# Self attention in a three-part Perceiver layer: the values' share token-major inside the logits' loop, and Ev turned by VectorE

## The chip, the cores and the metric

The kernel runs on one core of a Trainium2 chip. The metric is the device time of one execution in microseconds (us). Engines are written as in the profile: PE is TensorE (its weight loads are PEld), DVE is VectorE, ACT is ScalarE, POOL is GpSimd, SP is SyncE. L727 is line 727 of the kernel before.

## The reference

Three residual sub-layers on `x` (4 batches, 128 tokens, 512 channels, 16 heads of 32 channels), all in f32: a cross attention over 2048 context tokens whose softmax runs over the heads, a self attention with relative positions, and a cosine-like self attention with routed gates. Only the second is touched by the change:

```python
def _L0_attn_ref(x, Wq, Wk, Wv, Eq, Ek, Ev):     # x is layer-normalised
    r = jnp.arange(S)
    rel = jnp.clip(r[:, None] - r[None, :], -MAX_DIST, MAX_DIST) + MAX_DIST
    q, k, v = (proj(Wq), proj(Wk), proj(Wv))
    a_q, a_k, a_v = Eq[rel], Ek[rel], Ev[rel]
    content = jnp.einsum('bhld,bhmd->bhlm', q, k)
    rel_k = jnp.einsum('bhld,lmd->bhlm', q, a_k)
    rel_q = jnp.einsum('bhmd,lmd->bhlm', k, a_q)
    pos_pos = jnp.einsum('lmd,lmd->lm', a_q, a_k)
    logits = (content + rel_k + rel_q + pos_pos) * scale
    attn = jax.nn.softmax(logits, axis=-1)
    out = jnp.einsum('bhlm,bhmd->bhld', attn, v) + jnp.einsum('bhlm,lmd->bhld', attn, a_v)
    return out.transpose(0, 2, 1, 3).reshape(B, S, D)
...
x = x + _L0_attn_ref(_layernorm(x), ...)
x = x + _L0_ffn_ref(_layernorm(x), ...)
```

The second term of `out` is called Ev below: for every token position p, the attention weights of all heads and batches times a window of the table Ev.

## The kernel before

The kernel has three stages, one for each sub-layer. Within a stage the order of instructions is written out by hand (`manual_schedule`): every engine executes its own queue in the order of the program text, and semaphores between the engines are put in automatically. There is no planner, so what an engine does next is what the text says next, and an instruction that waits holds up everything behind it on its engine. Stage 1 (cross attention) lasts to about 650 us and isn't touched.

Stage 2 is the self attention. The 16 heads are handled in four chunks `c` of `NH` = 4 heads (128 channels), and every chunk head has its 4 batches side by side, so that one PSUM bank holds 4 x 128 = 512 columns. First q, k, v and the two relative terms are computed; `rk` and `lg` hold them. Then a loop over `c` does this for each chunk:

- `logits(c)` (L683): PE turns 16 blocks of `rk` into PSUM (L687) and adds the q k products (L700). It takes four banks, the only four of its pool, so logits of the next chunk wait until the joins have read them.
- `join(c)` (L713): four DVE additions of a PSUM bank to `lg` (L716).
- `largest(c, i)` (L720): the negated row maximum, one DVE instruction for each head.
- `exponentials_of(c, i)` (L724): four ACT exponentials for each head with their row sums (L727).
- `softmax(c, i)` (L731): a DVE reciprocal (L733) and a POOL multiplication by it (L734).
- `transposed(c, i)` (L738): PE turns the four 128x128 blocks of a head into a PSUM bank (L742), and DVE (heads 0 and 1) or ACT (heads 2 and 3) copies it to `eT` (L743).

In the loop before, `logits(c + 1)` stands first in pass c, and the turns of chunk c - 1 are spread behind the joins of chunk c + 1. After the loop, `attend(c)` (L750) makes the values' share of each chunk channel-major: it first turns four blocks of the residual `x1` into the bank (L753) and then adds 16 products with 32 columns of `v` as weights and 128 columns of `eT` moving (L765), four column groups of PE beside each other. DVE copies the bank to `oT` (L773). Then Ev: 128 positions, each one product with a 32-column window of the table as weights and the 64 columns of `eT` at that position moving (L818), in four groups of 32 positions. Its result has channels of one head on 32 partitions and positions, heads and batches along the free side, so it is brought into `oT` in strips of 32 partitions: half by ACT copies to `oev` (L835) with a POOL addition (L839), half by DVE additions (L833). Finally 16 PE turns bring `oT` back to tokens (L843), and `layernorm_T` (L145) takes the statistics (L157, L158), normalises (L161, L169, L165), turns the result into `xT` (L214, L215) and copies the new residual to `x1` (L207).

Stage 3 begins with `queries(b)` (L888) for each batch b: four 512-column products (L227), a DVE addition of the bias row (L891) and an ACT square (L893); `lengths(b)` (L896) and `normalised(b)` (L900) follow. Its bias rows are loaded by POOL's queue (L52) once stage 2's memory is free. After the queries come `keys` (L220) and the rest of the gated attention.

PSUM has eight banks. In stage 2, four belong to the logits (freed after the loop), three to `bank`, one to `bank_z`; stage 3 splits them into four for `bank_l` and four for `bank`.

Of the kernel before, what the change touches and what calls it, by code (L numbers as in the profile page):

```python
# [9 lines left out]
F32 = mybir.dt.float32  # L10
AF = mybir.ActivationFunctionType
# [5 lines left out]
def perceiver_layer(ctx: ExitStack, tc: tile.TileContext, a: dict, out: bass.AP):  # L17
# [7 lines left out]
    nc = tc.nc  # L25
# [210 lines left out]
    with s1:  # L236
# [11 lines left out]
        def bank(n):  # L248
            return ps_g.tile([P, 512], F32, tag="ps", name=f"ps_{n}")
# [318 lines left out]
    with ExitStack() as s2:  # L568
# [11 lines left out]
        def bank_z(n):  # L580
            return psz.tile([P, 512], F32, tag="psz", name=f"s2_{n}")
# [101 lines left out]
        def logits(c):  # L683
            ps, _ = banks(f"l{c}")
            for i in range(NH):
                for b in range(B):
                    nc.tensor.matmul(  # L687
                        ps[i][:, b * T : (b + 1) * T],
                        lhsT=rk[:, (c * NH + i) * B + b, :],
                        rhs=ident,  # L690
                        is_transpose=True,
                        start=(b == 0),
                        stop=False,
                        skip_group_check=True,
                    )
            for b in range(B):
                cols = slice(b * T, (b + 1) * T)
                for i in range(NH):
                    rows = slice(i * HD, (i + 1) * HD)
                    nc.tensor.matmul(  # L700
                        ps[i][:, cols],
                        lhsT=qT[rows, c, cols],
                        rhs=kT[rows, c, cols],
                        start=False,
                        stop=True,
                        skip_group_check=True,
                    )
            return ps
# [1 line left out]
        def of_head(c, i):  # L710
            return slice((c * NH + i) * B, (c * NH + i + 1) * B)

        def join(c, ps):  # L713
            for i in range(NH):
                fs = of_head(c, i)
                nc.vector.tensor_tensor(  # L716
                    lg[:, fs, :], ps[i].rearrange("p (b m) -> p b m", b=B), lg[:, fs, :], ALU.add
                )
# [9 lines left out]
                    lg[:, f, :], lg[:, f, :], AF.Exp, bias=nm[:, f : f + 1], accum_out=rs[:, f : f + 1]  # L728
                )

        def softmax(c, i):  # L731
            fs = of_head(c, i)
            nc.vector.reciprocal(rs[:, fs], rs[:, fs])  # L733
            nc.gpsimd.tensor_tensor(  # L734
                lg[:, fs, :], lg[:, fs, :], rs[:, fs].unsqueeze(2).to_broadcast([P, B, T]), ALU.mult
            )

        def transposed(c, i):  # L738
            ps = bank(f"t{c}_{i}")
            fs = of_head(c, i)  # L740
            for b in range(B):
                nc.tensor.transpose(ps[:, b * T : (b + 1) * T], lg[:, fs.start + b, :], ident)  # L742
            (nc.scalar.copy if i >= 2 else nc.vector.tensor_copy)(  # L743
                eT[:, fs, :], ps.rearrange("p (b l) -> p b l", b=B)
            )


        oT = one.tile([P, C, B, T], F32, tag="qT", name="oT2")

        def attend(c, eng):  # L750
            ps = bank_z(f"o{c}") if c % 2 else bank(f"o{c}")
            for b in range(B):
                nc.tensor.matmul(  # L753
                    ps[:, b * T : (b + 1) * T],
                    lhsT=x1[:, b, c * P : (c + 1) * P],
                    rhs=ident,
                    is_transpose=True,
                    start=(b == 0),
                    stop=False,
                    skip_group_check=True,  # L760
                )
            for b in range(B):
                for i in range(NH):
                    h = c * NH + i
                    nc.tensor.matmul(  # L765
                        ps[i * HD : (i + 1) * HD, b * T : (b + 1) * T],
                        lhsT=v[:, b, h * HD : (h + 1) * HD],
                        rhs=eT[:, h * B + b, :],
                        start=False,
                        stop=True,  # L770
                        skip_group_check=True,
                    )
            eng(oT[:, c].rearrange("p b l -> p (b l)"), ps)  # L773

        ps = logits(0)
        join(0, ps)
        for i in range(NH):
            largest(0, i)
        for c in range(C):
            if c + 1 < C:  # L780
                ps = logits(c + 1)
            for i in range(NH):
                exponentials_of(c, i)
            if c + 1 < C:
                join(c + 1, ps)
            for i in range(NH):
                if c + 1 < C:
                    largest(c + 1, i)
                softmax(c, i)
                if c:  # L790
                    transposed(c - 1, i)
        s2_loop.close()
        psq = s2.enter_context(tc.tile_pool(name="s2_psq", bufs=4, space=PSUM))

        def bank_q(n):
            return psq.tile([P, 512], F32, tag="psq", name=f"s2_{n}")


        nc.scalar.activation(small.tile([P, 1], F32, tag="rt", name="rt2"), eps, AF.Sqrt)
        attend(0, nc.vector.tensor_copy)  # L800
        attend(1, nc.vector.tensor_copy)
        for i in range(NH):
            transposed(C - 1, i)
            if i == 1:
                attend(2, nc.vector.tensor_copy)

        oev = one.tile([P, C * B, NG4, J8], F32, tag="kT", name="oev")  # L810
        by_8 = oT.rearrange("p c b (g n j) -> p (c b) g n j", g=NG4, j=J8)
        for n in range(NJ // J8):
            bk8 = bank_q(f"ev{n}")
            ps = bk8.rearrange("p (j f) -> p j f", f=NF)
            for j in range(J8):
                for g in range(NG4):
                    p = NJ * g + n * J8 + j
                    nc.tensor.matmul(  # L818
                        ps[g * HD : (g + 1) * HD, j, :],
                        lhsT=ev_win[:, T - 1 - p, :],  # L820
                        rhs=eT[:, :, p],
                        start=True,
                        stop=True,
                    )
            if n == 0:
                attend(C - 1, nc.vector.tensor_copy)
            for g in range(NG4):
                from_ = ps[g * HD : (g + 1) * HD].rearrange("p j (c i b) -> p i c b j", i=NH, b=B)
                for i in range(NH):
                    rows = slice(i * HD, (i + 1) * HD)  # L830
                    if n % 2:
                        to = oT[rows, :, :, g * NJ + n * J8 : g * NJ + (n + 1) * J8]
                        nc.vector.tensor_tensor(to, from_[:, i], to, ALU.add)  # L833
                    else:
                        nc.scalar.copy(  # L835
                            oev[rows].rearrange("p (c b) g j -> p c b g j", b=B)[:, :, :, g, :], from_[:, i]
                        )
            if n % 2 == 0:
                nc.gpsimd.tensor_tensor(by_8[:, :, :, n, :], by_8[:, :, :, n, :], oev, ALU.add)  # L839
        out_ps = [bank_q(f"out{b}") for b in range(B)]  # L840
        for b in range(B):
            for c in range(C):
                nc.tensor.transpose(out_ps[b][:, c * P : (c + 1) * P], oT[:, c, b, :], ident)  # L843
        xT = layernorm_T(out_ps, ps1, 2)

# [8 lines left out]
    with ExitStack() as s3:  # L854
# [121 lines left out]
        def attend(c, eng):  # L976
# [11 lines left out]
                    )  # L988
            eng(oT[:, c, :], ps)

        sqs = {0: queries(0)}
        for b in range(B):
            lengths(b, sqs[b])
            if b + 1 < B:
                sqs[b + 1] = queries(b + 1)
            normalised(b)
# [178 lines left out]
```

## Time and profile before

| what | value |
|---|---|
| median of 3 runs | 875.72 us (874.93 to 877.7) |
| the profiled execution | 875.97 us |
| its span, first to last instruction | 874.1 us |
| busy: PE, DVE, ACT, POOL | 830.6 (95%), 628.2 (72%), 436.5 (50%), 430.6 (49%) us |
| mean granted TensorE clock | 0.98 of full speed |
| first exponential of stage 2 | 732.25 us |
| Ev's products | 768.08 to 779.23 us |
| stage 3's queries on PE | 793.97 to 807.94 us |

Times inside the span are counted from its first instruction. Lines of the trace give start, duration, engine, source line, operation, output <- inputs, shapes and a count; in square brackets stands how long the engine was idle before it and what ended that. PE executes an f32 product in two records with a weight load each, so 16 products appear as x32; a turn (transpose) is one record. Busy shares are averages over stages that have different limits.

### The profile page before, as it was taken

The page shows a single profiled execution, that of the slowest core. Times are in us where ns is not written, and L with a number is a line of the kernel's source. Part 1 is how long each engine was busy: PE and PEld are TensorE (multiplying, and loading weights), DVE is VectorE, ACT ScalarE, POOL GpSimd, SP SyncE. Part 2 cuts the span into 40 slices and gives each one's busy share as a digit, 9 for nine tenths or more (in the row PEclk, how much of TensorE's full clock was granted, in tenths as well). Part 3 has the DMA queues.
Part 4 walks back from the last instruction along what each step waited for, and adds up shares of the span by engine and source line. Part 5 has one row for each costly group of instructions (what it writes and reads, how often), then busy time and mean ns, then how long its engine had stood idle before and what let it go on. Part 6 is the DMA issues. An engine that isn't in the chain of part 4 may idle for free. (4 is left out here: it accounts for less than half of the span.)

```text
span 874.1 us, 16373 instructions
## 1 busy us (share of the span) xinstructions
PE 830.6 (95%) x7061; PEld 447.9 (51%) x7061; DVE 628.2 (72%) x616; ACT 436.5 (50%) x721; POOL 430.6 (49%) x289
## 2 busy tenths in 40 slices
PE   9999999999999999999999999999898997779998
PEld 5454544554544545445445445544443466664564
DVE  2059788878888888888889888788861637556663
ACT  3357455564464554554554555644411736843671
POOL 1236666566656567575675665667500002512152
PEclk9999999999999999999999999999998998798999
DMA  8130010110101101010010101010100212001101
GB/s 300 50 124 2 1 49 1 49 49 1 50 1 49 49 2 49 1 49 13 37 49 1 49 1 49 1 36 15 49 28 21 96 50 98 1 2 51 49 1 49
DMA packets 10905, 35.53 MB, mean 41 GB/s; under 512 B 977, under 2 KB 1138, under 8 KB 8786
## 3 DMA queue, kind: packets, MB, share of 16 engines
q1 hardware_dynamic: 8402, 29.43, 9.7%
q10 hardware_dynamic: 1632, 3.15, 1.1%
q0 software_dynamic: 800, 1.93, 0.9%
q8 instruction: 55, 0.90, 0.4%
q14 instruction: 16, 0.13, 0.0%
HBM read 33.45 MB, written 1.05 MB: 39 GB/s over the span
## 5 line engine op out<-in xcount | busy, mean ns | idle before, releaser
L328 DVE TENSOR_TENSOR sg<-sg,stat 128x2048 f32<-128x2048 f32 x128 | 288.2, 2282 | 1.2
L337 ACT ACTIVATE sg<-sg 128x2048 f32<-128x2048 f32 x64 | 122.4, 1912 | 246.8 <-DVE sg L328 246.8
L227 PE MATMUL ps_v<-w_xattn_Wv,ct 128*128 128x512 f32 x512 | 231.5, 596 | 3.7 <-ACT v L274 3.7
L220 PE MATMUL ps_k<-ct,w_xattn_Wk 128*128 128x512 f32 x480 | 221.9, 605 | 0.8 <-ACT pos L142 0.8
L343 POOL TENSOR_TENSOR sm<-sm,sg 128x1024 f32<-128x1024 f32 x46 | 108.6, 2360 | 145.5 <-ACT sg L337 143.3
L307 DVE TENSOR_TENSOR mx<-mx,ps_s 128x1024 f32<-128x1024 f32 x96 | 117.2, 1221 | 78.1 <-ACT sg L298 65.9
L227 PEld LDWEIGHTS ps_v<-w_xattn_Wv,ct 128*128 128x128 f32 x512 | 95.8, 190 | 129.9 <-issue 113.5
L220 PEld LDWEIGHTS ps_k<-ct,w_xattn_Wk 128*128 128x128 f32 x480 | 86.2, 189 | 94.1 <-issue 86.1
L298 ACT COPY sg<-ps_s 128x1024 f32<-128x1024 f32 x128 | 124.2, 1020 | 7.2 <-DVE mx L305 3.5
L344 POOL TENSOR_TENSOR sm<-sm,sg 128x1024 f32<-128x1024 f32 x46 | 108.8, 2366 | 3.6
L275 POOL TENSOR_TENSOR v<-v,row_xattn_bv 128x512 f32<-128x512 f32 x64 | 81.6, 1276 | 40.0 <-ACT v L274 40.0
L734 POOL TENSOR_TENSOR lg<-lg,rs 128x512 f32<-128x512 f32 x16 | 16.3, 1041 | 120.9 <-issue 112.3
L285 PE MATMUL ps_s<-qT,kT 32*128 32x128 f32 x2048 | 75.7, 283 | 0.1
L372 PEld LDWEIGHTS pso<-sg,v 128*32 128x32 f32 x1920 | 48.8, 109 | 47.5 <-DVE mx L307 22.0
L285 PEld LDWEIGHTS ps_s<-qT,kT 32*128 32x128 f32 x2048 | 63.3, 186 | 18.0 <-issue 17.0
L372 PE MATMUL pso<-sg,v 128*32 128x128 f32 x1920 | 64.6, 276 | 3.7 <-DVE acc L385 2.1
L341 POOL TENSOR_TENSOR sm<-sg 128x1024 f32<-128x1024 f32 x16 | 37.9, 2366 | 45.3 <-ACT sg L337 45.2
L268 ACT ACTIVATE kT<-ps_k,bk 128x512 f32<-128x512 f32 x64 | 44.2, 694 | 10.4 <-PE ps_k L220 5.9
L274 ACT COPY v<-ps_v 128x512 f32<-128x512 f32 x64 | 36.4, 569 | 8.5 <-PE ps_v L227 8.4
L385 DVE TENSOR_TENSOR acc<-pso,acc 128x512 f32<-128x512 f32 x54 | 37.0, 684 | 3.9 <-PE pso L372 3.9
L305 DVE TENSOR_TENSOR mx<-sg,ps_s 128x1024 f32<-128x1024 f32 x16 | 19.5, 1220 | 27.3 <-ACT sg L298 27.3
L964 POOL TENSOR_TENSOR e<-e,rs 128x512 f32<-128x512 f32 x16 | 16.3, 1041 | 41.8 <-DVE rs L963 41.8
(208 smaller groups left out, 817.0 us busy)
## 6 DMA issues: line engine op xcount, KB each, us to landing
ct<-in_ctxT SPq DMA_DIRECT2D x15, 1024.0 KB, 4.9
ev_win<-in_tabv SPq DMA_DIRECT2D x1, 2048.0 KB, 7.1
w_xattn_Wk<-in_xattn_Wk ACTq DMA_DIRECT2D x4, 256.0 KB, 8.0
ct<-in_ctxT SPq DMA_DIRECT2D x4, 256.0 KB, 6.7
x<-in_x SPq DMA_DIRECT2D x4, 256.0 KB, 8.2
w_xattn_Wv<-in_xattn_Wv ACTq DMA_DIRECT2D x1, 1024.0 KB
w_xattn_Wq<-in_xattn_Wq SPq DMA_DIRECT2D x1, 1024.0 KB, 10.3
w_xattn_Wo<-in_xattn_Wo ACTq DMA_DIRECT2D x1, 1024.0 KB, 5.4
```

Of the source, the lines that this page charges most:

```text
L220: nc.tensor.matmul(ps, lhsT=w[:, k, c * P : (c + 1) * P], rhs=src[:, k, :], start=(k == 0), stop=(k == C - 1))
L227: nc.tensor.matmul(ps, lhsT=src[:, k, b * T : (b + 1) * T], rhs=w[:, k, :], start=(k == 0), stop=(k == C - 1))
L268: nc.scalar.activation(kT[n, c], ps, AF.Identity, bias=bk[:, c : c + 1])
L275: nc.gpsimd.tensor_tensor(v[n, b], v[n, b], bv_row, ALU.add)
L285: nc.tensor.matmul(ps[i][:, cols], lhsT=kT[n, c][rows, cols], rhs=qT[rows, c, cols], start=True, stop=True)
L298: nc.scalar.copy(sg[n, c][:, k * HALF : (k + 1) * HALF], pss[n, c][k])
L307: nc.vector.tensor_tensor(mxs[n], mxs[n], pss[n, c][k], ALU.max)
L328: nc.vector.tensor_tensor(g, g, stat[:, row, :].unsqueeze(1).to_broadcast([P, NH * B, T]), op)
L337: nc.scalar.activation(sg[n, c], sg[n, c], AF.Exp, scale=SCALE)
L343: eng.tensor_tensor(t, t, g[:, 0:HALF], ALU.add)
L344: eng.tensor_tensor(t, t, g[:, HALF:], ALU.add)
L372: nc.tensor.matmul(ps[i * HD : (i + 1) * HD, b * T : (b + 1) * T], lhsT=v[n, b][:, h * HD : (h + 1) * HD], rhs=sg[n, c][:, f * T : (f + 1) ...
```

## The change

- `attend` becomes token-major: for each head and batch one product with the 128 columns of `eT` as weights and 32 columns of `v` moving, into `bank_z`. It can be given some of the heads, and it no longer turns `x1`. `attended(c)` adds the bank to `x1` on DVE.
- In the loop, `logits(c + 2)` is issued near the end of pass c, after the turn of head 1. Of chunk c, heads 0 and 1 are turned in pass c and heads 2 and 3 at the start of pass c + 1; the values' share of chunk c - 1 stands in pass c between the turns of heads 0 and 1. The first joins and row maxima alternate. The last chunk's two late turns are copied by DVE, and its last softmax multiplication is on DVE.
- After the loop Ev's products go to one tile of four banks, the order of positions changed; twelve products with a constant tile follow on PE. DVE turns Ev for each batch in 32x32 blocks to token-major, straight out of PSUM; DVE (batch 0) or POOL (batches 1 to 3) adds it to `x1`. Statistics, root, reciprocal, offset and scaling are done batch by batch, the scaling on ACT.
- Stage 3 turns the normalised batches itself: `x_turned(b + 1)` stands behind `queries(b)`. Strips, `oev`, the 16 turns of `oT` and the copies to `x1` are gone.

```diff
-        def join(c, ps):
-            for i in range(NH):
+        def join(c, ps, heads=range(NH)):
+            for i in heads:
...
-        def softmax(c, i):
+        def softmax(c, i, eng=nc.gpsimd):
...
-        def attend(c, eng):
-            ps = bank_z(f"o{c}") if c % 2 else bank(f"o{c}")
...
+        def attend(c, heads=range(NH), ps=None):
+            if ps is None:
+                ps = bank_z(f"o{c}")
+            for i in heads:
+                for b in range(B):
                     h = c * NH + i
                     nc.tensor.matmul(
-                        ps[i * HD : (i + 1) * HD, b * T : (b + 1) * T],
-                        lhsT=v[:, b, h * HD : (h + 1) * HD],
-                        rhs=eT[:, h * B + b, :],
+                        ps[:, b * T + i * HD : b * T + (i + 1) * HD],
+                        lhsT=eT[:, h * B + b, :],
+                        rhs=v[:, b, h * HD : (h + 1) * HD],
+                        start=True,
+                        stop=True,
+                    )
+            return ps
+        def attended(c, ps):
+            xc = x1[:, :, c * P : (c + 1) * P]
+            nc.vector.tensor_tensor(xc, ps.rearrange("p (b d) -> p b d", b=B), xc, ALU.add)
...
+        act, dve = nc.scalar.copy, nc.vector.tensor_copy
+        ps = logits(0)
+        for i in range(NH):
+            join(0, ps, (i,))
+            largest(0, i)
+        ps = logits(1)
+        for c in range(C):
+            last = c + 1 == C
+            exponentials_of(c, 0)
+            if not last:
+                join(c + 1, ps)
+            softmax(c, 0)
+            if c:
+                transposed(c - 1, 2, dve if last else act)
+                transposed(c - 1, 3, dve if last else act)
+            if not last:
+                largest(c + 1, 0)
+            exponentials_of(c, 1)
+            softmax(c, 1)
+            transposed(c, 0, dve)
+            if not last:
+                largest(c + 1, 1)
+            if c:
+                po = attend(c - 1)
+            exponentials_of(c, 2)
+            softmax(c, 2)
+            if not last:
+                largest(c + 1, 2)
+            transposed(c, 1, dve)
+            exponentials_of(c, 3)
+            if c + 2 < C:
+                ps = logits(c + 2)
+            if c:
+                attended(c - 1, po)
+            if not last:
+                largest(c + 1, 3)
+                softmax(c, 3)
...
+        po = attend(C - 1, (0, 1))
+        transposed(C - 1, 2, dve)
+        softmax(C - 1, 3, nc.vector)
+        transposed(C - 1, 3, dve)
+        attend(C - 1, (2, 3), po)
+        attended(C - 1, po)
+        ev = psq.tile([P, NJ, NF], F32, tag="ev", name="ev")
+        for j in range(NJ):
...
+        for _ in range(12):
+            nc.tensor.matmul(ps, lhsT=warm, rhs=warm, start=True, stop=True)
+        def turn(b):
+            nc.vector.transpose(
+                turned[:, b, :].rearrange("p (h d) -> p h d", d=HD),
+                ev.rearrange("p j (h b) -> p b h j", b=B)[:, b],
+            )
+        def add(b, eng):
+            eng.tensor_tensor(x1[:, b, :], x1[:, b, :], turned[:, b, :], ALU.add)
+        def statistics(b):
+            nc.vector.bn_stats(st[:, b, :], x1[:, b, :])
+            nc.vector.bn_aggr(mv[:, b, :], st[:, b, :])
+            nc.scalar.activation(rstd[:, b : b + 1], mv[:, b, 1:2], AF.Sqrt, bias=eps)
+        def normalised(b):
...
+            nc.scalar.activation(xn[b], x1[:, b, :], AF.Identity, bias=nmr[:, one_], scale=rstd[:, one_])
+        turn(0)
+        add(0, nc.vector)
+        statistics(0)
+        turn(1)
+        add(1, nc.gpsimd)
+        normalised(0)
+        turn(2)
+        add(2, nc.gpsimd)
+        statistics(1)
+        turn(3)
+        add(3, nc.gpsimd)
+        normalised(1)
+        statistics(2)
+        normalised(2)
+        statistics(3)
+        normalised(3)
...
+        def x_turned(b):
+            ps = bank_l(f"xT{b}")
+            for c in range(C):
+                nc.tensor.transpose(ps[:, c * P : (c + 1) * P], xn[b][:, c * P : (c + 1) * P], ident)
+            nc.scalar.copy(xT[:, :, b * T : (b + 1) * T], ps.rearrange("p (c t) -> p c t", c=C))
+        x_turned(0)
         sqs = {0: queries(0)}
         for b in range(B):
+            if b + 1 < B:
+                x_turned(b + 1)
             lengths(b, sqs[b])
```

More of the change, by code (lines that the diff above doesn't have):

```diff
@@ L729, in exponentials_of, with transposed @@
                 )
-        def softmax(c, i):
+        def softmax(c, i, eng=nc.gpsimd):
             fs = of_head(c, i)
             nc.vector.reciprocal(rs[:, fs], rs[:, fs])
-            nc.gpsimd.tensor_tensor(
+            eng.tensor_tensor(
                 lg[:, fs, :], lg[:, fs, :], rs[:, fs].unsqueeze(2).to_broadcast([P, B, T]), ALU.mult
             )
-        def transposed(c, i):
+        def transposed(c, i, eng):
             ps = bank(f"t{c}_{i}")
@@ L742, in transposed @@
                 nc.tensor.transpose(ps[:, b * T : (b + 1) * T], lg[:, fs.start + b, :], ident)
[L743 to L748, printed above, removed]
-        def attend(c, eng):
-            ps = bank_z(f"o{c}") if c % 2 else bank(f"o{c}")
[L752 to L763, printed above, removed]
+            eng(eT[:, fs, :], ps.rearrange("p (b l) -> p b l", b=B))
@@ L764, in attend @@
+        def attend(c, heads=range(NH), ps=None):
[3 more added lines that the diff above has]
+                for b in range(B):
                     h = c * NH + i
                     nc.tensor.matmul(
-                        ps[i * HD : (i + 1) * HD, b * T : (b + 1) * T],
-                        lhsT=v[:, b, h * HD : (h + 1) * HD],
-                        rhs=eT[:, h * B + b, :],
-                        start=False,
-                        stop=True,
@@ L771, in attend @@
[L771 to L805, printed above, removed]
@@ L810, in perceiver_layer @@
[L810 to L821, printed above, removed]
+                        ps[:, b * T + i * HD : b * T + (i + 1) * HD],
@@ L824, in perceiver_layer @@
                     )
-            if n == 0:
-                attend(C - 1, nc.vector.tensor_copy)
-            for g in range(NG4):
[L828 to L844, printed above, removed]
+            return ps
+        def attended(c, ps):
+            xc = x1[:, :, c * P : (c + 1) * P]
+            nc.vector.tensor_tensor(xc, ps.rearrange("p (b d) -> p b d", b=B), xc, ALU.add)
@@ new lines, in perceiver_layer @@
+        s2_loop.close()
+        psq = s2.enter_context(tc.tile_pool(name="s2_psq", bufs=1, space=PSUM))
+        nc.scalar.activation(small.tile([P, 1], F32, tag="rt", name="rt2"), eps, AF.Sqrt)
+        po = attend(C - 1, (0, 1))
[6 more added lines that the diff above has]
+        for j in range(NJ):
+            for g in range(NG4):
+                nc.tensor.matmul(
+                    ev[g * HD : (g + 1) * HD, j, :],
+                    lhsT=ev_win[:, T - 1 - (NJ * g + j), :],
+                    rhs=eT[:, :, NJ * g + j],
+                    start=True,
+                    stop=True,
+                )
@@ new lines, in perceiver_layer @@
+        ps = bank("warm")[:, 0:P]
+        for _ in range(12):
+            nc.tensor.matmul(ps, lhsT=warm, rhs=warm, start=True, stop=True)
+        turned = one.tile([P, B, D], F32, tag="kT", name="evT")
+        def turn(b):
[3 more added lines that the diff above has]
+            )
+        st = small.tile([P, B, 6], F32, tag="st", name="st2")
+        mv = small.tile([P, B, 2], F32, tag="mv", name="mv2")
@@ new lines, in perceiver_layer @@
+        rstd = small.tile([P, B], F32, tag="rstd", name="rstd2")
+        nmr = small.tile([P, B], F32, tag="nmr", name="nmr2")
+        xn = [tmp.tile([P, D], F32, tag="xn", name=f"xn2_{b}") for b in range(B)]
+        def add(b, eng):
[4 more added lines that the diff above has]
+            nc.scalar.activation(rstd[:, b : b + 1], mv[:, b, 1:2], AF.Sqrt, bias=eps)
@@ new lines, in normalised @@
+        def normalised(b):
+            one_ = slice(b, b + 1)
+            nc.vector.reciprocal(rstd[:, one_], rstd[:, one_])
+            nc.vector.scalar_tensor_tensor(
+                nmr[:, one_], in0=mv[:, b, 0:1], scalar=-1.0, in1=rstd[:, one_], op0=ALU.mult, op1=ALU.mult
+            )
+            nc.scalar.activation(xn[b], x1[:, b, :], AF.Identity, bias=nmr[:, one_], scale=rstd[:, one_])
[4 more added lines that the diff above has]
+        add(1, nc.gpsimd)
@@ L989, in attend @@
             eng(oT[:, c, :], ps)
+        xT = tpool.tile([P, C, B * T], F32, tag="xT", name="xT2")
+        def x_turned(b):
[4 more added lines that the diff above has]
+        x_turned(0)
         sqs = {0: queries(0)}
         for b in range(B):
+            if b + 1 < B:
+                x_turned(b + 1)
             lengths(b, sqs[b])
```

## The prediction

> **What bounds the kernel now.** I read the page's slices first, then the chain of waits in order of time, then the timelines of single engines and the windows' granted clock between 715 and 812 us, where all edits lie. Stage 1 ends at 650 us, so its share of the busy time says nothing here.
>
> ```profile
> span 874.1 us, 16373 instructions
> ...
> PE   9999999999999999999999999999898997779998
> ...
> ACT  3357455564464554554554555644411736843671
> ...
> PEclk9999999999999999999999999999998998798999
> ```
>
> Each digit is a fortieth, 21.9 us: slices 33 to 35 (721 to 787 us) are the only ones where PE is not nearly full, and ACT takes over in slice 33. The profiled execution took 875.97 us, 1.87 more than its span and 0.25 more than the median of the three (875.72); the sum below is made against 875.97.
>
> ```profile
> 732.25 12.43 ACT lg L727 x64
> ...
> 768.08 2.52 PE s_ev L818 x60
> ...
> 774.60 0.28 DVE oT L833
> ...
> 784.36 1.10 PE s_out L843 x4
> ...
> 793.97 13.97 PE s_q L227 x32
> ```
>
> That is the chain (start, us, what; 64 counts each exponential and its accumulator read). The loop hangs on ACT's exponentials, the last at 761.1; the position products (Ev) run on PE from 768.08 to 779.23; then come strips on DVE (L833), turns, normalisation, and stage 3's queries from 793.97 to 807.94. From there on nothing is edited. So three marks decide: start of Ev, end of Ev, end of the queries.
>
> **The loop, part by part.** Prices, from the timelines (start, us, engine, line, [idle <-releaser]):
>
> ```profile
> 733.97 2.48 DVE L716 TENSOR_TENSOR lg<-s_l,lg 128x512 f32<-128x512 f32 x4
> 735.41 2.26 PE L687 MATMUL s_l<-ident,rk 128*128 128x128 f32 x16 [1.47 <-DVE lg L716]
> 738.75 0.66 PE L742 MATMUL s_t<-ident,lg 128*128 128x128 f32 x4
> 742.23 1.04 POOL L734 TENSOR_TENSOR lg<-lg,rs 128x512 f32<-128x512 f32 x1 [0.54 <-DVE rs L733]
> 771.12 1.08 PE L765 MATMUL s_o<-eT,v 128*32 128x128 f32 x32
> ```
>
> Four joins 2.4 (start to start); a logits group 3.34 (735.41 to 738.75); a head's turn 0.66; reciprocal (starts 741.98) plus POOL product (ends 743.27) 1.29; a largest or an eT copy on DVE 0.6 to 0.7.
>
> *The values' share.* Before, 16 products with 32 weight columns, four column groups side by side: 32 records, 1.08 us. After, eT is the weight (128 columns) and v moves 32 columns: again 32 records, but no two share the array. No row has this shape. From below it is bounded by the old 1.08; the nearest row with full f32 weights is the warming group of the start, of which a window holds
>
> ```profile
> 4.42:5.49 1.07, 1.07 (x10) 1.07 (x9) 1.00 1.08 374
> ```
>
> ten records in 1.07 us, 0.107 each, with as many weight loads. With 128 columns of weights per record I take 32 x 0.107 = 3.4; from above the same group's mean, 4.62/24 = 0.19, gives 6.2. [...]
>
> *The order.* Engines run their queues in order. In pass c, DVE now has: four joins of c+1, the first reciprocal of c, and only then the largest of c+1 and the eT copies. PE has: turns (c-1,2), (c-1,3), (c,0), the values' share of c-1, turn (c,1), logits c+2. So from the end of one logits group to the end of the next the steps follow each other: joins 2.4, reciprocal and product 1.29, turn 0.66, values' share A, turn 0.55, logits 3.34, some 0.05 of semaphore: 8.3 + A = 11.7 us. Before, logits c+1 stood in front of the turns on PE and the pass took 6.2 to 8.5 (exponentials of passes 0 to 3 begin at 732.25, 738.4, 746.9, 754.9). Nothing covers the difference: ACT's copies of turns (c-1,2), (c-1,3) stand between exponentials (c,0) and (c,1), and those turns wait behind the logits, so ACT stands still too.
>
> Worked through: joins and largest of pass 0 now alternate, a dependent pair costing 1.33, so exponentials start at 730.5 instead of 732.25, but the fourth join ends at 733.8 and logits 1 at 736.1 (before 733.9). Logits 2: joins to 738.5, product (0,0) 739.8, (0,1) 740.8, turn 741.5, logits 744.8. Logits 3: 744.8 + 11.7 = 756.5. Then: product (2,0) 760.3, turn 760.9, values 1 764.3, turn and copy (2,1) 765.6, the add into x1 and largest (3,3) 766.8, products (2,3) 768.1 and (3,0) 769.1, turn 769.8, values 2 773.2, turn and copy (3,1) and add 775.4, half of values 3 777.1, turn and copy (3,2) 778.4, reciprocal and product of (3,3) on DVE 779.3, turn 780.0, copy 780.7, rest of values 3 781.3. Ev starts at 781.3 rather than 768.08. It takes 256 x 0.0377 (7.21 us for 192) = 9.65 as before, without the 1.75 of values 3 in its midst: end 791.0 against 779.23, **+11.8**.
>
> Gone from PE are 16 x1 turns (about 2.6 us) and 16 output turns; they stood after the exponentials, so they are in the sum through the marks.
>
> **After Ev.** Removed: 32 strips on DVE (9.6 us, half beside PE), 32 on ACT, two POOL adds, four copies of x1. Added per batch: a 32x32 turn on DVE, an add, statistics, scaling. The turn is in no row; other 128x512 reads of PSUM on DVE, strided ones too (L634), take 0.69, single-input ones down to 0.66; bounds 0.5 and 1.3 (the POOL add), and I take 0.69. POOL's adds take 1.28 (L458). From Ev's end: turn, add, statistics, root of batch 0 to 2.7; turn 1 ends 3.0; POOL's adds at 4.35, 5.6, 7.3; statistics of batch 1 4.4, of 2 6.1 (behind batch 1's scale on DVE), of 3 7.6; the last root waits for ACT's scaling of batch 2 to 8.55; root, scale, offset 9.2; the last scaling 10.1. Stage 3's first xT copy is behind that on ACT: 10.6. So "each batch by itself" doesn't bring the first query forward by much: PE has batch 0's turn at 4.2 and waits. Then four queries of 3.43, with a new gap between: add 0.69, square 0.63 (ACT), copy of the next xT 0.59, semaphores: 2.0 each, three times. End 30.4 after Ev. The wait also costs clock:
>
> ```profile
> 659.08 5.80 PE L220 MATMUL s_q<-xT,w_attn_Wq 128*128 128x512 f32 x8 [0.83 <-ACT x L207]
> ```
>
> after stage 1's normalisation the first eight records took 5.8, not 3.43: 2.4 more (bounds 0 and 3.4). The twelve warming products end about 2.6 after Ev, 8 us too early. Sum 32.8 against 807.94 - 779.23 = 28.7: **+4.1**. POOL's row loads now queue behind its last add (7.3); bq is landed some 4 us later, before 14.1 where it is used. The exponentials' table in stage 3 and the output weights move along.
>
> **The clock in the loop.**
>
> ```profile
> 741.87:745.28 3.41, 0.00 (x0) 1.00 0.00 0
> 745.28:748.69 3.41, 3.39 (x16) 0.50 0.00 0
> 748.69:752.11 3.41, 3.20 (x50) 1.00 0.00 0
> ```
>
> (window, length, PE busy and records, clock.) An empty window was followed by half clock, a full one by full clock. The same addition made for the old order ends the exponentials at 759.1 where the trace has 761.2, so half-clock stretches and bank waits cost **2.1** there; I carry that over. [...]
>
> Sum: 875.97 + 11.8 + 4.1 + 2.1 = **894.0 us**.
>
> **Rivals.**
> - *Faster.* The pass fits under ACT: 730.5 + 64 x 0.386 + four copies 2.0 = 757.2, tail 3.6 (product, turn, copy, products), Ev 760.8 to 770.5, queries to 803.3: 871.3, with stage 3 ahead of the last scaling on ACT about 866. It decides where the time from logits to logits is under 7.2. For it: ACT starts 1.75 earlier and is what the chain names. Against: 8.3 even with the values' share free. 0.09.
> - *Cheap values' share* (1.1): logits 3 at 754.2, Ev 772.9 to 782.6: 3.4 + 4.1 + 2.1 = 885.6; about 881 if the xT copies pass the scaling. 0.15.
> - *Half clock through the loop*: weights with 32 moving columns keep the array mostly empty. All turns, logits and values at 1.5 times their time end Ev at about 805 instead of 791: 908; at half clock nearly throughout beyond 915. 0.2.
> - *Forecast case*, 888 to 902: 0.56.
>
> **How the numbers follow.** Predicted 894. Range 881 to 912: the lower end is the cheap share, the upper takes in half clock at 1.5; outside are the faster case and the worst clock, about 0.2. What this kernel's measurement tells from no change is about 0.3%. Faster 0.09; of the cheap share's 0.15, where the xT copies also pass the scaling and the clock stays up, 0.03 is put within 0.3%: same 0.03; the rest, slower 0.88.
>
> **What would show it.** Right: values' share groups of 32 records at 3.4 us or more; logits to logits near 12; ACT idle some 4 us before each xT-like copy of turns in passes 1 and 2; Ev starting near 781; first query 10 to 11 us after Ev, at half clock; gaps near 2 between queries. Wrong: values' share near 1.1; exponentials ending by 762; Ev starting before 768; queries starting within 6 us of Ev.

## The result, and the profile after

The changed kernel takes 907.36 us (median of four runs, 907.13 to 907.62), the kernel before 875.72: 1.0352 times as long, with a 95% interval of 1.0335 to 1.037. It is slower by some 32 us, 13 more than forecast, and still inside the range. It is the rival "half clock through the loop" that came true, not the forecast case. The span of the profiled execution is 905.6 us.

The page first, the slices that were shown of before:

```profile
span 905.6 us, 16294 instructions
...
PE   9999999999999999999999999998889967886998
...
ACT  3358446446454555555554545544116335303570
PEclk9999999999999999999999999999989967579999
```

A slice is now 22.6 us. ACT is ahead of PE in no slice of the stage any more (before it was in slice 34, 743 to 765 us; the prediction says 33), and PEclk falls to 6, 7, 5, 7 where before it never went below 7. Next the chain of waits (start, us, what):

```profile
763.89 2.48 DVE lg L716 x4
...
768.29 5.70 PE s_o L752 x32
...
780.19 6.67 PE s_o L752 x32
...
799.76 9.50 PE ev L821 x233
...
816.87 3.85 DMA row_ffn_bq<-in_ffn_bq
...
822.73 5.41 PE s_q L227 x8
...
839.49 6.87 PE s_k L220 x16
```

The chain held 32 exponentials with their accumulator reads in a row before. It now goes from joins (L716) to values' shares (L752) and back. Ev ends at 809.23 instead of 779.23, 30.0 us later; the queries end 30.3 us behind it instead of 28.7. So nearly all of the loss lies ahead of Ev's end. PE's own timeline through the loop:

```profile
744.04 2.55 PE L687 MATMUL s_l<-ident,rk 128*128 128x128 f32 x16
...
751.96 6.69 PE L752 MATMUL s_o<-v,eT 128*128 128x32 f32 x32
758.46 1.09 PE L742 MATMUL s_t<-ident,lg 128*128 128x128 f32 x4
759.34 3.41 PE L687 MATMUL s_l<-ident,rk 128*128 128x128 f32 x16
...
768.12 5.87 PE L752 MATMUL s_o<-v,eT 128*128 128x32 f32 x32
...
779.98 6.88 PE L752 MATMUL s_o<-v,eT 128*128 128x32 f32 x32
```

A values' share takes 5.9 to 6.9 us, 0.18 to 0.21 a record, where 3.4 was forecast. A turn takes 1.09 where 0.66 was its price. Both suggest a slower clock, and the windows (length, PE busy and records, granted clock; the two last columns are the DMA engines' share and GB/s) say that it was half; the first line reaches from 732.25, where the exponentials of before began, to the start of Ev, the last covers Ev's first 3.5 us:

```profile
732.25:799.80 67.55, 51.36 (x336) 0.60 0.00 1
779.44:782.85 3.41, 3.41 (x19) 0.50 0.02 5
782.85:786.27 3.42, 3.42 (x18) 0.50 0.00 0
799.80:803.30 3.50, 3.50 (x100) 0.50 0.02 5
```

and of before, the loop up to the last exponential:

```profile
732.25:761.20 28.95, 19.87 (x206) 0.84 0.01 2
```

One thing stands out: from 769.2 to 803.4 us the clock stays at half although PE is busy in 28.72 of these 34.2 us, and in the second and third line it is busy without a break. Turns, on the other hand, did bring the clock back here, as they did in the window from 745.28 to 748.69 before: all 18 records of the first of these two windows are turns.

```profile
758.99:762.40 3.41, 3.41 (x18) 0.50 0.00 0
762.40:765.81 3.41, 2.48 (x43) 1.00 0.00 0
```

### The profile page after: what moved, and what is told of

Same layout as the page of the kernel before. It is cut to its first block, busy times and chain, and to the rows that moved or that the text cites. A ratio compares the mean times of both kernels' runs of the same rounds, so it can differ in the third digit from the quotient of the medians.

```text
span 905.6 us, 16294 instructions
## 1 busy us (share of the span) xinstructions
PE 853.6 (94%) x7053; PEld 471.7 (52%) x7053; DVE 624.3 (69%) x595; ACT 427.5 (47%) x687; POOL 430.7 (48%) x289
## 5 line engine op out<-in xcount | busy, mean ns | idle before, releaser
L268 ACT ACTIVATE kT<-ps_k,bk 128x512 f32<-128x512 f32 x64 | 44.2, 694 | 11.3 <-PE ps_k L220 6.0
```

Source lines behind the costliest of these rows:

```text
L268: nc.scalar.activation(kT[n, c], ps, AF.Identity, bias=bk[:, c : c + 1])
```

## The experiments

Theory after the result: the values' share itself is what holds the clock down, by its 32 moving columns; the clock makes it 6.7 us instead of 3.7, and through the order on PE that is passed on to the logits. Rivals: the price of the weights alone, whatever the clock; the order alone; the tail.

Marks of different runs are compared by their distance from the end of an earlier step, because some executions reach the first logits group some 3 us later (727 instead of 722 to 724 us), for a reason that lies ahead of every edit. The kernel before was measured anew beside each group of experiments, with medians from 875.72 to 878.11 us. The ratios below are against the one beside them; differences in us between experiments are good to some 2 us.

**1. More moving columns (e1_wide).**

```diff
-                        ps[:, b * T + i * HD : b * T + (i + 1) * HD],
+                        ps[:, b * T : (b + 1) * T],
                         lhsT=eT[:, h * B + b, :],
-                        rhs=v[:, b, h * HD : (h + 1) * HD],
+                        rhs=v[:, b, c * P : (c + 1) * P],
```

> The changed kernel, but every product of the values' share moves 128 columns of v instead of 32 into its bank (each head overwrites the last, so the attention output is left wrong); the weights, the number of records and the order are the same. Theory (clock): 32 moving columns leave the array so empty that the granted clock falls to half, and at half clock a weight load paces each record at 0.21 us. A record with 128 moving columns took 0.107 us at full clock in the warming group, no more than its weight load, so fuller records cost nothing and keep the clock up: values' share groups of 3.4 to 4 us instead of 5.7 to 6.7, Ev's end 8 to 18 us earlier, 889 to 899 us in all. Rival (weight loads take 0.2 us for this shape whatever the clock): groups stay at 5.7 to 6.7 us, 905 to 910 us.

Measured: 894.84 us, 1.0194 [1.0169, 1.0218] of before. Four times the moving columns make the kernel 12.5 us faster. Two shares on PE's timeline, and two windows at the second of them:

```profile
754.90 3.74 PE L752 MATMUL s_o<-v,eT 128*128 128x128 f32 x32
...
766.19 5.37 PE L752 MATMUL s_o<-v,eT 128*128 128x128 f32 x32
```

```profile
766.70:770.11 3.41, 3.41 (x18) 0.50 0.01 2
770.11:773.52 3.41, 2.32 (x21) 0.99 0.00 0
```

Set the first of them beside 782.85 to 786.27 of the changed kernel: the same 18 records of a share at half clock, the same unbroken busy time. Behind the 18 of 128 columns the clock was back in the next window (0.99); behind the 18 of 32 columns it was not (0.50 from 786.27 to 789.68), nor behind 779.44 to 782.85, where four turns stand among them. At full clock (1.00 from 754.90 to 758.50) the share of 128 columns took 3.74 us; experiment 4 has one of 32 columns at full clock, 3.76. So the width cost nothing in time at full clock, and in windows of equal busy time it decided over the clock.

**2. The operands swapped back (e2_swapped).** v as weights, 32 columns; eT moves; loop, order and tail stay.

```diff
-                        ps[:, b * T + i * HD : b * T + (i + 1) * HD],
-                        lhsT=eT[:, h * B + b, :],
-                        rhs=v[:, b, h * HD : (h + 1) * HD],
+                        ps[i * HD : (i + 1) * HD, b * T : (b + 1) * T],
+                        lhsT=v[:, b, h * HD : (h + 1) * HD],
+                        rhs=eT[:, h * B + b, :],
```

> The changed kernel with the operands of the values' share swapped back: 32 columns of v as weights, 128 columns of eT moving, four column groups; the result is channel-major and is added to the token-major residual as if it weren't, so the output is wrong. Theory (the share's price is the loss, its records and the clock that they cost): groups near 1.1 us at full and 1.9 at half clock, Ev ends at 783 to 788 instead of 809, 881 to 887 us in all. Rival (the order of the loop alone makes the loss): Ev ends after 795, 893 us or more.

Measured: 889.5 us, 1.014 [1.0124, 1.0157], between the two expectations. The share took 2.46 us, not 1.1. In the kernel before, where 32 records took 1.08 us, neighbouring products go to different column groups; here the heads are the outer loop and neighbours go to the same one. That this is the cause is a guess; no run tests it by itself. From 750.2 us on the clock stayed full, even behind a window in which PE was busy for only about half of the time, with turns and products of 128 moving columns:

```profile
770.67:774.09 3.42, 1.83 (x15) 1.00 0.00 0
774.09:777.50 3.41, 2.46 (x33) 1.00 0.02 5
```

So even with 32 weight columns and the clock up (1.00) the changed kernel stays 12.6 us slower than before; that much lies in the loop's order, the tail, and a share of 2.46 instead of 1.08 us.

**3. The new tail on the old loop (e3_tail_only).** The old loop and the old values' share; 16 turns of oT to token-major and their copies stand amid Ev; from Ev's end on everything is as in the change.

```diff
+        for j in range(NJ):
+            if j == 8:
+                attend(C - 1, nc.vector.tensor_copy)
+            if j == 16:
+                for b in range(B):
+                    token_major(b)
```

> The loop and the values' share of the kernel before; after it the changed kernel's part: Ev in one tile, turned by VectorE in 32x32 blocks for each batch, batch by batch into stage 3. So that the residual is token-major, the 16 turns of oT stay, in the middle of Ev's products, and ACT copies them to x1. Correct result. Theory (the part after Ev gives no gain: the first query comes early, but bias row, gaps and clock give it back): Ev ends near 782 (16 turns later than 779.2), the queries end 29 to 31 us after that, 877 to 881 us. Rival (that part is a gain by itself, the loss is all in the loop): queries end under 26 us after Ev, 870 to 875 us.

Measured: 878.54 us, 1.0024 [1.0002, 1.0047]; its runs fell into two groups, near 877 and near 882.5, and the profile is of the second. The tail brings nothing by itself, as the theory had it. Its trace names two reasons (DVE, then PE):

```profile
796.14 0.69 DVE L924 TENSOR_TENSOR q<-s_q,row_ffn_bq 128x512 f32<-128x512 f32 x1 [1.94 <-DMA row_ffn_bq<-in_ffn_bq]
```

```profile
798.07 5.40 PE L227 MATMUL s_q<-w_ffn_WqT,xT 128*128 128x512 f32 x8 [3.48 <-ACT xT L1030]
805.44 3.70 PE L227 MATMUL s_q<-w_ffn_WqT,xT 128*128 128x512 f32 x8 [1.54 <-ACT xT L1030]
```

The first query starts 5.65 us after Ev, but its bias row comes 1.94 us too late, the copy of the next xT stands behind on ACT, and the second query takes 5.40 us instead of 3.70. In the changed kernel, where it took 5.40 too, the clock granted during it was 0.68 (0.50 from 823.84 to 827.25).

**4. Logits ahead of the values' share (e4_logits_first).** The addition into x1 moves one pass on.

```diff
-            if c:
-                po = attend(c - 1)
+            if c > 1:
+                attended(c - 2, po)
             exponentials_of(c, 2)
...
             if c + 2 < C:
                 ps = logits(c + 2)
             if c:
-                attended(c - 1, po)
+                po = attend(c - 1)
```

> The changed kernel with another order in the loop: the values' share of chunk c-1 stands behind the logits of c+2 on PE instead of in front of the turn and the logits, and its addition on VectorE one pass later. Correct result. Theory (part of the loss is the order: the share lies on the way from one logits group to the next): logits to logits 9 to 11 us instead of 16.2, last exponential before 770 instead of 778.5, Ev's end 5 to 12 us earlier, 895 to 902 us. Rival (PE is bound by its records at half clock, wherever they stand): within 3 us of 907.

Measured: 900.96 us, 1.0271 [1.0253, 1.0289], 6.4 us less than the change. The ends of logits 1, 2 and 3 are at 736.2, 746.1 and 756.0: 9.9 us apart both times, where the changed kernel has 9.8 and 16.2. PE's timeline, the first two shares:

```profile
755.94 3.76 PE L752 MATMUL s_o<-v,eT 128*128 128x32 f32 x32
...
764.91 6.97 PE L752 MATMUL s_o<-v,eT 128*128 128x32 f32 x32
```

The share that follows the logits runs at full clock (1.00 from 755.94 to 759.50), the next one, after 3.16 us of waiting and one turn, at half (0.50 from 764.90 to 771.80). The order costs 6.4 us, but mostly together with the slow share, as the next run shows.

**5. Both (e6_wide_order).** The edits of 1 and 4 together.

> Two earlier edits together: the values' share moves 128 columns of v instead of 32 (the output of the attention's values is thereby not the reference's: each head's columns are overwritten by products of the next), and it stands behind the logits of chunk c+2 on TensorE, its addition one pass later. Alone they gave 894.8 and 901.0. Theory A (two separate costs, the clock and the place in the order): both gains add, 907.4 - 12.5 - 6.4 = 888.5, range 886.5 to 890.5; logits-to-logits about 9.9 us both times, the values' share 3.6 to 3.9 us for most groups. Theory B (the place cost only because the share ran at half the clock; at full clock it stands in TensorE's idle time): 893 to 895.5, no gain over the wide one alone.

Measured: 893.87 us, 1.0196 [1.0181, 1.0211], against 1.0194 for the wide share alone. The time lies in theory B's range: with the clock mostly up (0.85 from 733.9 to 788.5 us) the place of the share makes no difference in the medians that could be measured. In the two profiled executions the way from the first logits to Ev is 61.5 us against 63.7 in experiment 1, while experiment 4 shortened it from 75.6 to 70.4. So most of the 6.4 us of experiment 4 are the half clock, seen a second time; some 2 us for the place itself are not excluded.

**6. More work for PE, the share as it is (e7_filler).** If too little work in the windows is the cause, work that nobody needs should help, with the share left at 32 columns.

```diff
+        def filler(n):
+            ps = bank("fill")[:, 0:P]
+            for _ in range(n):
+                nc.tensor.matmul(ps, lhsT=warm, rhs=warm, start=True, stop=True)
...
+            filler(8)
             transposed(c, 0, dve)
...
+        filler(8)
         po = attend(C - 1, (0, 1))
```

> The changed kernel with five warming groups more (8 products of warm by warm each, 16 records, about 2 us at full clock), one in each pass ahead of turn (c,0), where TensorE waits 2.75 to 4.2 us for GpSimd's product, and one ahead of the last values' share. They add work to TensorE and take none away. Theory (the clock falls because the windows around the shares hold too little work by its measure; idle time ahead of a share is part of it): at least half of the 34.1 us of half clock from 769.2 on go, values' shares take 3.7 to 5.5 us instead of 5.9 to 6.9, Ev starts 5 to 10 us earlier; time 896 to 902 beside 907.4. Rival (the shares of 32 moving columns pull the clock down themselves, whatever stands before them, so only wider products help): shares stay at 5.9 to 6.9 us, and the added groups cost what doesn't fit into the idle time; 906 to 911.

Measured: 897.29 us, 1.0231 [1.0201, 1.0262]. 80 added records make the kernel 10.1 us faster. PE's timeline, and the clock of the loop:

```profile
746.82 1.95 PE L770 MATMUL s_fill<-warm 128*128 128x128 f32 x16
749.52 0.66 PE L742 MATMUL s_t<-ident,lg 128*128 128x128 f32 x4 [0.75 <-POOL lg L734]
750.01 3.66 PE L752 MATMUL s_o<-v,eT 128*128 128x32 f32 x32
```

```profile
732.25:790.26 58.01, 49.16 (x408) 0.79 0.01 2
```

The first two shares take 3.66 us each, right behind their groups, which stand in PE's wait for POOL and delay nothing (POOL still ends the wait). Later the clock falls again, from 764.8 to 775.1 and twice more before Ev (from 778.5 and 785.3), and the last two groups run at half clock themselves (3.62 us at 769.86, 3.54 at 778.60, where the one at 746.82 took 1.95). The first fall settles whether the wait is needed:

```profile
761.42:764.84 3.42, 3.42 (x33) 1.00 0.03 7
764.84:768.25 3.41, 1.79 (x9) 0.50 0.00 0
```

The first window is busy without a break at full clock; all but one of its records are a values' share, and the clock is half in the next. So here narrow products lost the clock without any wait. Filling the wait or widening the products brought most of it back: 0.79 here and 0.85 in experiment 1 (733.20 to 790.58), where the changed kernel had 0.60.

**7. The bias row early (e5_row_early).** The changed kernel; the row is asked for just before Ev, into its own place.

```diff
+        fbq_row = load_row("ffn_bq", D, rowp)
         ev = psq.tile([P, NJ, NF], F32, tag="ev", name="ev")
...
-        fbq_row = load_row("ffn_bq", D, one)
```

> The changed kernel, with one edit in the third stage's start: the row of the queries' bias (row_ffn_bq) is asked for by GpSimd just before Ev, into a place of its own, and no longer behind GpSimd's last addition of stage 2. In the changed kernel's trace the addition of the bias to the first query (q) waited 2.29 us for this row, and the second query then ran at half the clock after 3.79 us of idle (5.40 us instead of 3.70). Theory (the row is on the path): the first addition starts at once after its query, the idle before the second query falls to about 1.5 us, that query takes about 3.7 us, and the queries end 2.3 to 4.0 us earlier after Ev, about 26.5 to 28 us instead of 30.3; time 903 to 905 beside 907.4 for the changed kernel. Rival (the row was hidden, as the forecast had it; something else holds the second query): within 1 us of 907.4, queries' end at about 30 us after Ev.

Measured: 904.5 us, 1.0318 [1.0304, 1.0333], 2.9 less than the change. PE's timeline:

```profile
820.73 3.70 PE L227 MATMUL s_q<-w_ffn_WqT,xT 128*128 128x512 f32 x8 [1.53 <-ACT xT L1032]
```

The second query starts 2.0 us earlier and takes 3.70 us instead of 5.40; the queries end 26.3 us after Ev instead of 30.3. The row was on the path.

**8. All edits of the changed kernel that keep its share and its output (e8_all).** Edits 4, 6 and 7 and the turns amid the queries, shown below.

> The changed kernel with all edits that keep its values' share in 32 moving columns and its output: the share behind the logits of chunk c+2 (901.0 alone), the queries' bias row asked for before Ev (904.5 alone), the xT turns amid the queries, and the five warming groups. Theory: if the warming groups stand in for the wider products, the loop takes what it took with wide products and this order (893.9), and the tail gives 7.7 us back as it did with the old loop (878.5 to 872.9 measured: 5.6): 886 to 889. Rival (the groups don't hold the clock): the loop as with the order alone, 901.0 less 5.6 to 7.7: 893 to 896. Either way it stays slower than the kernel before (876): the shares' full weights, 3.7 us each where the old ones took 1.1 and 1.7 with their inputs, and five turns between products that follow each other.

Measured: 891.36 us (888.01 to 896.29), 1.0168 [1.014, 1.0196], between the two, a little nearer to the second; the executions spread over both, and the profiled one (888.45) lies in the first. Its full shares took 3.76, 4.96 and 3.76 us. So the change, with everything mended that was found, still costs 1.7%: Ev starts 32.8 us behind the end of the last logits (755.0 to 787.9), where the kernel before needs 17.7 (750.4 to 768.1). What is left is in that stretch: four shares with full weights, 16.9 us of PE's time, with turns between them that wait for their products.

**9. The old loop with the mended tail (f1_tail_new).** Experiment 3, the row early, and each turn of xT in the middle of the query before it:

```diff
+            for k in range(C):
+                nc.tensor.matmul(
+                    ps, lhsT=xT[:, k, b * T : (b + 1) * T], rhs=fwq[:, k, :], start=(k == 0), stop=(k == C - 1)
+                )
+                if k == 1 and amid is not None:
+                    x_turned(amid)
```

> The combination of the old loop (the values' share transposed, as before, turned back by 16 TensorE transposes amid Ev) with the new tail, which gave 878.5, and two edits of the tail: the bias row of the queries is asked for just before Ev; and each xT turn of batch b+1 stands in the middle of the query of batch b on TensorE, with its ScalarE copy ahead of the square of query b. Theory: in the run that gave 878.5 the four queries took 3.7, 5.4, 3.7, 3.7 us with idle of 3.5, 1.5, 1.5 us between them, from 5.65 us after Ev; without the idle they run through, 4 x 3.7 + 3 x 0.6 = 16.6 us, so the queries end about 22.3 us after Ev instead of 30.0: 7.7 us less, 870.8, range 869.5 to 873; faster than the kernel before (875.7) by 0.3 to 0.7%. Rival (the tail is bound by the normalisation's chain on VectorE and ScalarE, batch by batch, not by the queries' order): gaps near 1 us remain, 874 to 878.

Measured: 872.86 us, 0.996 [0.9949, 0.9972]. PE's timeline, the first two queries and the turn between them:

```profile
788.00 3.60 PE L925 MATMUL s_q<-w_ffn_WqT,xT 128*128 128x512 f32 x4 [0.73 <-ACT xT L1036]
791.44 0.60 PE L1035 MATMUL s_xT<-ident,xn 128*128 128x128 f32 x4
791.88 3.60 PE L925 MATMUL s_q<-w_ffn_WqT,xT 128*128 128x512 f32 x8
```

The queries follow each other without a break and end 23.0 us after Ev. The first four records took 3.60 us, as long as eight of the second query: half clock. It is faster than before, by 3.5 us rather than 5.

**10. Two values' shares in the loop's idle time (f2_loop_too).** The kernel of 9, and:

```diff
+                if c >= 2 and i == 2:
+                    attend(c - 2, nc.vector.tensor_copy)
...
-        attend(0, nc.vector.tensor_copy)
-        attend(1, nc.vector.tensor_copy)
```

> The kernel of the run before this one in the list, and the values' shares of chunks 0 and 1 moved from behind the loop into its passes 2 and 3 (behind the third turn of the pass, in TensorE's idle time of 1.9 to 3.9 us before the fourth turn), with VectorE copying all four turned heads in the last pass. In the profile of before these two shares took 759.22 to 763.79 behind the loop, with Ev starting at 768.08. Theory: the shares keep the old operand order (128 moving columns, 1.1 us of products and 0.7 us of turned inputs each), so they fit; Ev starts about 2 to 3 us earlier, 868 to 869.5. Rival: the share in pass 2 delays the fourth turn and ScalarE's copy and exponentials behind it by up to 1 us, and TensorE's work of the last pass is no less, so nothing is won: 870 to 872.5.

Measured: 868.53 us (866.59 to 872.27), 0.9918 [0.9897, 0.9938]: the fastest of all, 0.8% faster than before and 39 us faster than the change. PE's timeline, and the clock up to Ev:

```profile
752.13 1.08 PE L766 MATMUL s_o<-eT,v 128*32 128x128 f32 x32
...
765.10 2.52 PE L822 MATMUL ev<-eT,ev_win 128*32 128x64 f32 x64 [0.73 <-ACT eT L744]
...
784.41 1.98 PE L925 MATMUL s_q<-w_ffn_WqT,xT 128*128 128x512 f32 x4 [0.73 <-ACT xT L1036]
```

```profile
732.25:765.10 32.85, 23.18 (x306) 0.95 0.03 10
```

The spans of 9 and 10 differ by 5.2 us. Of these 3.1 lie ahead of the loop (the first logits group at 726.83 against 723.73), 1.6 in the first query (3.60 us for its first four records at half clock against 1.98), and only 0.5 between the first logits and Ev. So it is not shown that the two moved shares bring more than the half microsecond, nor that they are what kept the clock up.

## Why the prediction was right in sign and short in size

**The order of the loop: right.** The forecast's chain (joins, reciprocal and product, turn, values' share, turn, logits) is the one that the trace names, and ACT's idle time before the copies of the late turns is there: 5.53 and 8.93 us, where 4 were expected. Exponentials no longer set the end.

**The price of the values' share: right at full clock.** 32 x 0.107 = 3.4 us was taken from the warming group; at full clock it took 3.66 to 3.76, in experiments 1, 4, 6 and 8. A record of the share took some 0.117 us at full clock (3.74 and 3.76 by 32), a tenth above the 0.107 of the warming group, with 128 moving columns as with 32; at half clock one took 0.21 (6.69 by 32).

**The clock: this is the step that failed.** The forecast carried over 2.1 us from before, on the ground that a full window had brought the clock back there. That window held turns; windows as full of the new products left the clock at half (0.50 from 779.44 on), or brought it there (0.50 from 764.84 on in experiment 6). The forecast gave half clock through the loop as a rival, 908 us at 0.2 with Ev ending near 805; measured are 907.36 and 809.2. That the rival's time fits to 0.6 us is partly luck: with the 2.1 added, its Ev ends at 807.1, which is 2.1 too early, and its tail is 2.5 too long. The marks show how the error grows:

| mark, us | forecast | measured | error added |
|---|---|---|---|
| end of logits 1 | 736.1 | 737.9 | 1.8 |
| logits 1 to 2 | 8.7 | 9.8 | 1.1 |
| logits 2 to 3 | 11.7 | 16.2 | 4.5 |
| logits 3 to start of Ev | 24.8 | 35.8 | 11.0 |
| Ev | 9.65 | 9.54 | -0.1 |
| Ev's end to the queries' end | 32.8 | 30.3 | -2.5 |

The first four add 18.4 us, against the 2.1 carried over. Less the 2.1, which they contain, and the 2.6 of the last two, that is 13.7; the forecast was 13.4 short of the median (13.6 of the profiled execution). That the 18.4 are mostly clock is shown by the two runs that brought it back in opposite ways, wider products (12.5 us) and added work (10.1), and by the order's 6.4 us all but vanishing with it. The clue was in the forecast's own text, in the rival's reason, the 32 moving columns (how empty they leave the array no run shows), and it was set aside because the windows shown held only turns of 128 columns.

In the stretches read here one clock holds for 3.41 us or a multiple of it: before, half from 745.28 to 748.69; after, full from 762.40 to 769.22 and half from there to 803.36. A busy window did not always bring it back: those from 779.44 to 786.27 are busy throughout and stay at half clock. With the clock up the kernel would have been near the forecast; an estimate is the 894 to 897 us of experiments 1, 5 and 6, where it was mostly up (0.85, 0.85 and 0.79 in the loop). Nor does the time that the profile shows as busy decide it: the 3.42 us of experiment 6 lost the clock, the 1.83 us of experiment 2 kept it. That the moving columns of a window decide fits all of these; no run measures how many it takes.

**The tail: +1.6 instead of +4.1, by errors in both directions.** The first query came 5.6 us after Ev, not 10.6, which the forecast had named as a sign of being wrong (within 6 us). The scalings came as forecast, the last ending 10.2 us after Ev (10.1), but ACT's copy of the first xT stands between those of batches 0 and 1, not behind the last (ACT):

```profile
814.16 0.59 ACT L1031 COPY xT<-s_xT 128x512 f32<-128x512 f32 x1 [0.80 <-PE s_xT L1030]
...
818.61 0.81 ACT L861 ACTIVATE xn<-x,nmr,rstd 128x512 f32<-128x512 f32 x1 [0.48 <-DVE nmr L858]
```

In the program text the copy comes behind all four scalings, so across the border of the two stages the queue did not follow the text; how that came about no run shows. The first query also ran at full clock (1.00 from 814.80 to 818.50), and the price of a slow one fell on the second instead (5.40 for 3.70 us at a mean clock of 0.68, 1.7 more where 2.4 was taken). These lines of the changed kernel show why (DVE, then PE):

```profile
809.29 0.72 DVE L836 STREAM_TRANSPOSE evT<-ev 128x512 f32<-128x512 f32 x1 [8.80 <-PE ev L821]
...
820.80 0.69 DVE L925 TENSOR_TENSOR q<-s_q,row_ffn_bq 128x512 f32<-128x512 f32 x1 [2.29 <-DMA row_ffn_bq<-in_ffn_bq]
```

```profile
814.80 3.70 PE L227 MATMUL s_q<-w_ffn_WqT,xT 128*128 128x512 f32 x8 [0.73 <-ACT xT L1031]
...
822.73 5.40 PE L227 MATMUL s_q<-w_ffn_WqT,xT 128*128 128x512 f32 x8 [3.79 <-ACT xT L1031]
```

The forecast had seen that POOL's row loads queue behind its last addition, but called them hidden since "bq is landed ... before 14.1 where it is used". That 14.1 followed from the late first query. The row landed 11.5 us after Ev, and with the query earlier it was the wait. So the landing was priced about right (11.3 was expected); one wrong place in a queue hid that it was on the path. Of the small prices, VectorE's turn of 128x512 took 0.68 to 0.72 us (0.69 taken) and the later gaps between queries 2.0, as taken.

## What to carry to other kernels

Price a new PE product twice, at full and at half clock, and then ask which clock its own windows will earn: here products with 128 weight columns and 32 moving ones lost the clock behind 3.42 us without a break (experiment 6) and left it at half with PE busy for 28.72 of 34.2 us, and a step that is on the path at half clock delays what is queued behind it (logits 2 to 3 took 16.2 us where 11.7 was forecast). When a transfer is called hidden, write down the moment at which its user would be ready if every other estimate were too late. Where a mended part of a change (here the tail, with the row early and the turns amid the queries) gains, put it on the old version of the rest before giving up both.

## What the runs showed of the hardware

- 32 f32 records with 128 weight columns took 3.76 us with 32 moving columns (experiment 4) and 3.74 with 128 (experiment 1) at full clock, but behind windows of 3.41 us at half clock, busy without a break, full clock was back only with the wider ones (0.99 against 0.50). At full clock a window of 3.42 us filled with the narrow ones lost it (experiment 6), and one busy for 1.83 us with 128 moving columns kept it (experiment 2).
- Added products (80 records of 128 by 128) made a kernel 10.1 us faster; the clock granted between 732.25 and the start of Ev was 0.79 instead of 0.60. The tile that they multiply holds zeros.
- Ev, with 32 weight columns and 64 moving ones in four column groups, did not slow down at half clock: a window of 3.41 us at 0.50 (from 799.95) holds 103 of its records, the next one at 1.00 holds 104. At half clock turns took 1.65 times as long (1.09 for 0.66), values' shares 1.83 times (6.88 for 3.76).
